# The row of sender scores of a graph-attention layer, turned in 32x32 squares by VectorE

## The chip, the cores and the metric

The kernel runs on one core of one Trainium2 chip. The time is that of one execution on the device, in microseconds (us); three runs of the kernel before were taken, and their median counts. The profile is of one further execution; its span is what the hardware profiler saw on that core. Busy times, waits and durations below are of that execution.

The engines of the core are named as the profile names them: PE is TensorE (matmuls and transposes), PEld its loading of weights, DVE is VectorE, ACT is ScalarE, POOL is GpSimd, SP is SyncE, which here only issues DMA transfers.

## The reference

Four graph layers run one after another over 32 graphs of 512 nodes with 128 features each; each layer normalizes, computes and adds its result to x. Layer 0 is a graph convolution, layer 1 a gated graph network with five steps, layers 2 and 3 are graph attention. The change touches only layers 2 and 3. Layer 3, cut to what matters:

```python
h = jnp.einsum('bnf,fo->bno', x, w)
e_src = jnp.einsum('bno,o->bn', h, a_src)
e_dst = jnp.einsum('bno,o->bn', h, a_dst)
e = jax.nn.leaky_relu(e_src[:, :, None] + e_dst[:, None, :], negative_slope=NEG_SLOPE)
mask = (a > 0)[None, :, :]
e = jnp.where(mask, e, -jnp.inf)
alpha = jax.nn.softmax(e, axis=-1)
out = jnp.einsum('bij,bjo->bio', alpha, h)
```

Layer 2 is the same with an ELU behind it. For each graph, one of the two scores must stand along the free dimension, as a row of 512 numbers that is the same on all 128 partitions, while the other stands as one number per partition. The kernel takes exponentials of scores first, so that the leaky ReLU of a sum becomes a maximum of two factors.

## The kernel before

The whole program is a list of operations, each with an engine, an estimated cost and a due time. A planner orders them ahead of time with these estimates; it tries sixteen settings of its ordering rule and keeps the one that ends first by its own estimates. Each engine then runs its operations in that fixed order, waiting on semaphores where data or buffers need it.

```python
def run(self):
    ...
    best = min(self.ends, key=lambda end: self.attempt(uses, *end))
    self.attempt(uses, *best)
    ...
    for o in self.order:
        o.emit()
```

The buffers that the change touches, and some of their neighbours:

```python
P = 128
W = 32
Q = P // W
NEAR = 4
...
"bank": tiles(8, TOKENS, "bank", psum),
...
"h_gat": tiles(3, [P, C, D + 3], "h_gat"),
"four": tiles(2, [Q, P], "four"),
"row": tiles(2, [P, N], "row"),
"line": tiles(4, [C, Q, W], "line", dram),
"e": tiles(2, [P, C, N], "e"),
```

`four` and `row` lie in the on-chip memory, `line` in device memory, `bank` in the matmul accumulator memory. C is 4, N is 512 and D is 128.

An attention layer of one graph makes the head tile `h_gat`: per node 128 features and three exponentials of scores in columns 128 to 130. Matmuls give features and scores (line 678), ACT takes the exponentials (line 680), and DVE multiplies the features by one of them (line 688). For the last four graphs ("near") other operations are used; those are not changed.

```python
def gat(b, l, due):
    ...
    near = b >= B - NEAR
    ...
    for a, q in enumerate(qs):
        ...
        op("PE", 2 * MM1, due + 1.5, heads, r=[gT, w_aug[l]], w=[*qs, h] if a == 0 else [q])
        op("ACT", 0.1, due + 1, lambda qt=qt, ht=ht: nc.scalar.activation(ht()[:, :, D:D + 3], qt()[:, :, D:D + 3], AF.Exp),
           r=[q], w=[h[2 + a]])
        if near:
            ...
        else:
            op("DVE", 0.335, due + 1.5, lambda qt=qt, ht=ht: nc.vector.tensor_mul(
                ht()[:, :, :D], qt()[:, :, :D], ht()[:, :, D:D + 1].to_broadcast([P, 2, D])), r=[q, h[2 + a]], w=[h[a]])
    exps = [h[2], h[3]]
```

Then the scores of column 130 are turned into a row. For the 28 graphs that are not near, PE transposes the four columns into four partitions of a bank (line 705), ACT copies them (line 707), one DMA writes them to `line` (line 708) and a second reads `line` back as a row on all partitions (line 710). DVE then makes the weighted mask `e` (line 713), and PE multiplies with it (line 733).

```python
    if near:
        ...
    else:
        pr, four, line = Val("bank"), Val("four"), Val("line")
        op("PE", 0.12, due + 1.5, lambda: nc.tensor.transpose(flat(pr.t)[:Q, :P], h.t[:, :, D + 2], ident.t),
           r=[*exps, ident], w=[pr, four])
        op("ACT", 0.22, due + 1.5, lambda: nc.scalar.copy(four.t, flat(pr.t)[:Q, :P]), r=[pr], w=[four])
        op("SP", 0.4, due + 1.5, lambda: nc.sync.dma_start(
            line.t.rearrange("c q i -> q c i"), four.t.rearrange("q (c i) -> q c i", c=C)), r=[four], w=[line], delay=2.5)
        op("SP", 0.4, due + 1.5, lambda: nc.sync.dma_start(
            row.t, line.t.rearrange("c q i -> (c q i)").unsqueeze(0).to_broadcast([P, N])), r=[line], w=[row, e], delay=7)
    for j in range(C):
        op("DVE", 0.68, due + 3, lambda j=j: nc.vector.scalar_tensor_tensor(
            e.t[:, j, :], row.t, h.t[:, j, D + 1:D + 2], maskT[l].t[:, j, :], op0=ALU.max, op1=ALU.mult),
           r=[row, h[2 + j // 2], maskT[l]], w=[e[j]])
```

Two layers and 28 graphs make 56 such rows.

Of the kernel before, what the change touches and what calls it, by code (L numbers as in the profile page):

```python
# [15 lines left out]
P = 128  # L16
# [3 lines left out]
W = 32  # L20
Q = P // W
# [23 lines left out]
class Plan:  # L45
# [8 lines left out]
    def op(self, engine, cost, due, emit, r=(), w=(), delay=None):  # L54
        o = Op(engine, cost, due, emit, self.DELAY[engine] if delay is None else delay)
        o.id = len(self.ops)
        before = {}
        for items, writes in ((r, False), (w, True)):
            for item in items:
                v, parts = item if isinstance(item, tuple) else (item, None)  # L60
                parts = range(len(v.writers)) if parts is None else [parts]
                if v not in o.vals:
                    o.vals.append(v)
                    v.uses += 1
                for c in parts:
                    before.update((p.id, p) for p in v.writers[c])
                    if writes:
                        before.update((p.id, p) for p in v.readers[c])
        for items, writes in ((r, False), (w, True)):
            for item in items:  # L70
                v, parts = item if isinstance(item, tuple) else (item, None)
                for c in range(len(v.writers)) if parts is None else [parts]:
                    if writes:
                        v.writers[c], v.readers[c] = [o], []
                    else:
                        v.readers[c].append(o)
        before.pop(o.id, None)
        for p in before.values():
            p.then.append(o)
        o.waits = len(before)  # L80
        self.ops.append(o)
# [86 lines left out]
def gnn_stack(ctx: ExitStack, tc: tile.TileContext, a: dict, out: bass.AP):  # L168
    nc = tc.nc
    x, adj = a["x"], a["adj"]  # L170
    B, N, D = x.shape
    C = N // P
# [6 lines left out]
    def tiles(n, shape, name, pool=sb, dtype=F32):  # L179
        return [pool.tile(shape, dtype, name=f"{name}_{next(serial)}") for _ in range(n)]  # L180

    def flat(t):
        return t.rearrange("p c k -> p (c k)")
# [18 lines left out]
        "hv": tiles(2, TOKENS, "hv"),  # L202
        "gT": tiles(2, [P, Q, W * C], "gT"),
        "h_gat": tiles(3, [P, C, D + 3], "h_gat"),
        "four": tiles(2, [Q, P], "four"),
        "row": tiles(2, [P, N], "row"),
        "line": tiles(4, [C, Q, W], "line", dram),
        "e": tiles(2, [P, C, N], "e"),
# [9 lines left out]
    op = plan.op  # L218
# [3 lines left out]
    def fixed(shape, name, parts=1, dtype=F32):  # L222
        v = Val(None, parts)
        v.t = tiles(1, shape, name, dtype=dtype)[0]
        return v
# [13 lines left out]
    ident = fixed([P, P], "ident")  # L239
# [8 lines left out]
    for c in range(C):  # L248
        e, q = (("SP", nc.sync), ("ACT", nc.scalar))[c % 2]
        op(e, 0.45, -1001, lambda c=c, q=q: q.dma_start(adj_sb.t[:, c, :], adj[c * P:(c + 1) * P, :]),  # L250
           w=[adj_sb[c]], delay=3.6)
    xs = []
    for b in range(B):
        v = Val("x", C)
        op("SP", 0.95, max(-995 + b, STEPS * b - 20) if b >= 8 else -995 + b, lambda v=v, b=b: nc.sync.dma_start(v.t, x[b].rearrange("(c p) d -> p c d", p=P)),
           w=[v], delay=3)
# [23 lines left out]
    for c in range(C):  # L280
        p = Val("bank")

        def turn_adj(c=c, p=p):
# [5 lines left out]
           r=[adj_sb[c]], w=[deg[c]])  # L289
# [17 lines left out]
    for m in range(C):  # L307
        op("DVE", 0.7, -797, lambda m=m: nc.vector.scalar_tensor_tensor(
            anT.t[:, m, :], adjT.t[:, m, :], dinv.t[:, m:m + 1], flat(drow.t), op0=ALU.mult, op1=ALU.mult),
           r=[adjT, dinv, drow], w=[anT[m]])  # L310
        op("DVE", 0.26, -797, lambda m=m: nc.vector.scalar_tensor_tensor(
            block(anT.t, m), ident.t, dinv2.t[:, m:m + 1], block(anT.t, m), op0=ALU.mult, op1=ALU.add),
           r=[ident, dinv2], w=[anT[m]])
# [19 lines left out]
    for l in (2, 3):  # L333
# [13 lines left out]
        for c in range(C):  # L347
            op("SP", 0.4, 4 + l, lambda l=l, c=c, far=far: nc.sync.dma_start(
                maskT[l].t[c * W:(c + 1) * W], far.t[:, :, c, :].rearrange("q i n -> i q n")),
               r=[far], w=[maskT[l][c]], delay=2.2)  # L350
# [33 lines left out]
    for k, u, half in (("w4", "u3", True), ("w3", "u3", True), ("w5", "u5", False)):  # L384
        gate_b[k] = fixed([P, 1], "gate_b" + k)
        op("DVE", 0.1, -14, lambda k=k, u=u: nc.vector.tensor_add(gate_b[k].t, raw["b" + k].t, raw["b" + u].t),
           r=[raw["b" + k], raw["b" + u]], w=[gate_b[k]])
# [4 lines left out]
    for i, l in enumerate((2, 3)):  # L392
        p = Val("bank")
        op("PE", 0.3, -9, lambda i=i, l=l, p=p: nc.tensor.matmul(p.t[:, 0, :2], gats.t[:, i, :], a_pair[l].t, start=True, stop=True),
           r=[gats, a_pair[l]], w=[p])
# [259 lines left out]
    def gat(b, l, due):  # L655
        xb, y, gT, h = xs[b], Val("y", C), Val("gT"), Val("h_gat", 4)
# [3 lines left out]
        if near:  # L660
# [4 lines left out]
               r=[pT], w=[gT])  # L665
# [6 lines left out]
        for a, q in enumerate(qs):  # L672
# [3 lines left out]
            def heads(a=a, qt=qt):  # L676
# [4 lines left out]
               r=[q], w=[h[2 + a]])  # L681
# [8 lines left out]
        exps = [h[2], h[3]]  # L690

        row, e = Val("row"), Val("e", C)
        if near:
            pr = Val("bank")

            def spread():
                for k in range(Q):
                    nc.tensor.transpose(pr.t[:, k, :], h.t[:, k, D + 2:D + 3].to_broadcast([P, P]), ident.t)
            op("PE", C * TURN, due + 2, spread, r=[*exps, ident], w=[pr, row])
            op("ACT", A, due + 2, lambda: nc.scalar.copy(  # L700
                row.t.rearrange("p (c q i) -> p c q i", c=C, q=Q), pr.t.rearrange("p q (c i) -> p c q i", c=C)),
               r=[pr], w=[row, e])
        else:
            pr, four, line = Val("bank"), Val("four"), Val("line")
            op("PE", 0.12, due + 1.5, lambda: nc.tensor.transpose(flat(pr.t)[:Q, :P], h.t[:, :, D + 2], ident.t),  # L705
               r=[*exps, ident], w=[pr, four])
            op("ACT", 0.22, due + 1.5, lambda: nc.scalar.copy(four.t, flat(pr.t)[:Q, :P]), r=[pr], w=[four])
            op("SP", 0.4, due + 1.5, lambda: nc.sync.dma_start(
                line.t.rearrange("c q i -> q c i"), four.t.rearrange("q (c i) -> q c i", c=C)), r=[four], w=[line], delay=2.5)
            op("SP", 0.4, due + 1.5, lambda: nc.sync.dma_start(  # L710
                row.t, line.t.rearrange("c q i -> (c q i)").unsqueeze(0).to_broadcast([P, N])), r=[line], w=[row, e], delay=7)
        for j in range(C):
# [3 lines that stand above are left out]
# [31 lines left out]
        if l == 2:  # L747
# [3 lines left out]
               r=[xb], w=[v])  # L751
            op("DVE", V, due + 4, lambda: nc.vector.scalar_tensor_tensor(flat(xb.t), flat(n.t), 1.0, flat(v.t), op0=ALU.min, op1=ALU.add),
               r=[n, v], w=[xb])
# [4 lines left out]
    for b in range(0, B, 2):  # L758
        gcn((b, b + 1), STEPS * b - 10)
        ggnn((b, b + 1), STEPS * b)  # L760
        for i in range(2):
            gat(b + i, 2, STEPS * (b + i) + LANES * (STEPS - 1) + 3)
            gat(b + i, 3, STEPS * (b + i) + LANES * (STEPS - 1) + 8)
# [32 lines left out]
```

The softmax here doesn't subtract the row's maximum and nothing guards it: scores larger than these inputs give would overflow.

## Time and profile before

| what | value |
|---|---|
| median of three runs | 1648.0 us (1646.48 to 1648.28) |
| span of the profiled execution | 1645.1 us |
| PE busy | 1620.7 us (99%) |
| DVE busy | 1373.5 us (83%) |
| ACT busy | 722.0 us (44%) |
| POOL busy | 144.6 us (9%) |
| mean granted clock of TensorE | 0.999 of full speed |

Busy time is the union of an engine's instructions, so that two matmuls that overlap in the pipeline are counted once. The table of stages gives, for stretches of the span, the busy time of each engine and in brackets the number of instructions in the stretch. In the table of groups a line holds the source line, the engine, the operation, the tiles written and read, their shapes and the count; behind the first bar stand the total busy time in us and the mean duration in ns, behind the second the idle time of the engine just before these instructions and what ended it. The chain that ended last is followed from the last instruction back to whatever released it.

### The profile page before, as it was taken

The page shows a single profiled execution, that of the slowest core. Times are in us where ns is not written, and L with a number is a line of the kernel's source. Part 1 is how long each engine was busy: PE and PEld are TensorE (multiplying, and loading weights), DVE is VectorE, ACT ScalarE, POOL GpSimd, SP SyncE. Part 2 cuts the span into 40 slices and gives each one's busy share as a digit, 9 for nine tenths or more (in the row PEclk, how much of TensorE's full clock was granted, in tenths as well). Part 3 has the DMA queues.
Part 4 walks back from the last instruction along what each step waited for, and adds up shares of the span by engine and source line. Part 5 has one row for each costly group of instructions (what it writes and reads, how often), then busy time and mean ns, then how long its engine had stood idle before and what let it go on. Part 6 is the DMA issues. An engine that isn't in the chain of part 4 may idle for free.

```text
span 1645.1 us, 23871 instructions
## 1 busy us (share of the span) xinstructions
PE 1620.7 (99%) x7306; PEld 1159.8 (71%) x7306; DVE 1373.5 (83%) x3881; ACT 722.0 (44%) x1629; POOL 144.6 (9%) x136
## 2 busy tenths in 40 slices
PE   8999999999999999999999999999999999999997
PEld 5666666777767677776776677767777777666776
DVE  8977587888878898888888898888888887788887
ACT  4643353534345443544534444353443534443433
POOL 2200010110101110000100100110000000000000
PEclk9999999999999999999999999999999999999999
DMA  5433253444535344453434535334363422434100
GB/s 148 109 73 72 53 127 93 104 106 105 124 78 136 90 106 106 102 134 86 113 95 100 129 90 142 87 94 113 91 143 76 114 68 72 122 91 103 46 20 26
DMA packets 381312, 159.81 MB, mean 97 GB/s; under 512 B 206976, under 2 KB 362752, under 8 KB 381184
## 3 DMA queue, kind: packets, MB, share of 16 engines
q1 hardware_dynamic: 380896, 157.77, 39.4%
q8 instruction: 58, 0.95, 0.2%
q14 instruction: 70, 0.57, 0.1%
q10 hardware_dynamic: 288, 0.52, 0.1%
HBM read 87.30 MB, written 70.89 MB: 96 GB/s over the span
## 4 chain that ended last, share of the span: by engine, by line
PE 94%; DVE 4%; DMA 1%; issue 0%; ACT 0%; SPq 0%; DVEq 0%
PE bank L516 34%; PE bank L733 12%; PE bank L603 8%; PE bank L604 8%; PE bank L617 8%; PE bank L610 8%; PE bank L618 8%; PE bank L678 3%; PE bank L572 1%; PE bank L722 1%; DVE e L713 1%; DVE st L406 1%; PE bank L705 0%; PE bank L448 0%; DVE y L432 0%
## 5 line engine op out<-in xcount | busy, mean ns | idle before, releaser
L413 POOL TENSOR_TENSOR rstd<-ve,mhalf 128x4 f32<-128x4 f32 x128 | 142.8, 1117 | 1473.4 <-DVE ve L411 1166.1
L516 PE MATMUL bank<-made,S 128*128 128x256 f32 x1128 | 270.3, 380 | 1.6 <-DVE S L504 0.7
L516 PEld LDWEIGHTS bank<-made,S 128*128 128x128 f32 x1128 | 217.3, 196 | 42.2 <-issue 18.6
L733 PEld LDWEIGHTS bank<-h_gat,e 128*128 128x128 f32 x1792 | 208.2, 192 | 17.4 <-issue 14.8
L521 ACT COPY half<-bank 128x256 f32<-128x256 f32 x282 | 104.6, 371 | 246.6 <-PE bank L516 239.1
L733 PE MATMUL bank<-h_gat,e 128*128 128x129 f32 x1792 | 209.0, 275 | 0.0
L606 ACT ACTIVATE r<-bank,gate_bw 128x512 f32<-128x512 f32 x160 | 109.6, 685 | 205.2 <-PE bank L604 186.5
L713 DVE SCALAR_TENSOR_TENSOR e<-row,h_gat,maskT 128x512 f32<-128x512 f32 x256 | 182.7, 742 | 0.0
L608 DVE SCALAR_TENSOR_TENSOR rh<-r,hT 128x512 f32<-128x512 f32 x160 | 109.9, 687 | 76.5 <-ACT r L606 75.6
L622 DVE TENSOR_TENSOR hv<-hv,hT 128x512 f32<-128x512 f32 x160 | 109.6, 685 | 75.9 <-ACT hv L620 75.3
L620 ACT ACTIVATE hv<-bank,gate_bw 128x512 f32<-128x512 f32 x160 | 109.5, 684 | 126.7 <-PE bank L618 125.6
L610 PE MATMUL bank<-m,wT 128*128 128x512 f32 x320 | 163.8, 593 | 0.0
L617 PE MATMUL bank<-m,wT 128*128 128x512 f32 x320 | 163.7, 593 | 0.0
L603 PE MATMUL bank<-m,wT 128*128 128x512 f32 x320 | 163.5, 592 | 0.0
L618 PE MATMUL bank<-rh,wT 128*128 128x512 f32 x320 | 163.4, 592 | 0.0
L604 PE MATMUL bank<-hT,wT 128*128 128x512 f32 x320 | 163.4, 592 | 0.0
L516 PE MATMUL bank<-adjT,h 128*128 128x256 f32 x640 | 161.6, 380 | 0.6 <-ACT h L423 0.3
L529 DVE TENSOR_TENSOR m<-half,bank 128x256 f32<-128x256 f32 x282 | 116.1, 413 | 33.2 <-ACT half L521 15.7
L516 PEld LDWEIGHTS bank<-adjT,h 128*128 128x128 f32 x640 | 121.2, 196 | 26.7 <-issue 11.3
L612 ACT ACTIVATE z<-bank,gate_bw 128x512 f32<-128x512 f32 x160 | 109.3, 683 | 53.8 <-PE bank L610 51.5
L406 DVE BATCH_NORM_STATS2 st<-x 128x6 f32<-128x128 f32 x512 | 121.5, 279 | 1.5 <-DMA x<-in_x_dram 0.6
L423 ACT ACTIVATE y<-x,off,rstd 128x128 f32<-128x128 f32 x240 | 104.5, 485 | 26.9 <-DVE off L420 25.0
(117 smaller groups left out, 2182.5 us busy)
## 6 DMA issues: line engine op xcount, KB each, us to landing
far<-sq SPq DMA_DIRECT2D x936, 64.0 KB
h<-far SPq DMA_DIRECT2D x248, 128.0 KB
gT<-far SPq DMA_DIRECT2D x56, 256.0 KB
row<-line SPq DMA_DIRECT2D x56, 256.0 KB
x<-in_x_dram SPq DMA_DIRECT2D x32, 256.0 KB
out_dram<-x SPq DMA_DIRECT2D x32, 256.0 KB
h<-far SPq DMA_DIRECT2D x28, 256.0 KB
hT<-far SPq DMA_DIRECT2D x104, 64.0 KB
```

The source lines that it names most:

```text
L406: op("DVE", 0.21, due, lambda c=c: nc.vector.bn_stats(st.t[:, c, :], xb.t[:, c, :]), r=[xb[c]], w=[st[c]])
L413: op("POOL", 1.0, due, lambda: nc.gpsimd.tensor_tensor(rstd.t, ve.t, mhalf.t, ALU.pow), r=[ve, mhalf], w=[rstd])
L516: nc.tensor.matmul(low(r), u[:, l, :], factors[k][0]()[:, l, :], start=fresh and l == 0, stop=l == 1, skip_group_check=not fresh)
L529: op("DVE", HV, due - 5, lambda: nc.vector.tensor_add(out(), u.t, low(t)), r=[u, t], w=[o])
L603: nc.tensor.matmul(flat(gate.t), gates.t[:, 0, :], flat(m.t), start=True, stop=False)
L604: nc.tensor.matmul(flat(gate.t), gates.t[:, 1, :], flat(hT.t), start=False, stop=True)
L608: op("DVE", V, due - 5, lambda: nc.vector.scalar_tensor_tensor(flat(rh.t), flat(r.t), 1.0, flat(hT.t), op0=ALU.add, op1=ALU.mult), r=[r, h ...
L610: op("PE", MM, due + 0.3, lambda: nc.tensor.matmul(flat(gate.t), gates.t[:, 2, :], flat(m.t), start=False, stop=True, skip_group_check=Tru ...
L617: nc.tensor.matmul(flat(cand.t), gates.t[:, 3, :], flat(m.t), start=True, stop=False)
L618: nc.tensor.matmul(flat(cand.t), u5T.t[:, 0, :], flat(rh.t), start=False, stop=True)
L713: op("DVE", 0.68, due + 3, lambda j=j: nc.vector.scalar_tensor_tensor(e.t[:, j, :], row.t, h.t[:, j, D + 1:D + 2], maskT[l].t[:, j, :], op ...
L733: nc.tensor.matmul(pt()[:, c, :D + 1], e.t[:, j, i * P:(i + 1) * P], h.t[:, j, :D + 1], start=(j == 0), stop=(j == C - 1))
```

## The change

One PE transpose and one ACT copy per row give way to one DVE instruction. DVE turns each 32x32 square of its operand by itself. It gets the last 32 columns (99 to 130) of each of the four slices of the head tile, 128 partitions by 4 x 32 numbers. Column 130, the score, is the last of its square, so it becomes the last row of each turned square, on partitions 31, 63, 95 and 127. Each of those four partitions then holds 128 scores side by side, and the first DMA takes these four partitions alone. The tile `four` grows from 4 x 128 to 128 x 4 x 32 numbers. The instruction reads feature columns too (99 to 127), whose turned values nobody uses, so it names the whole head tile as its input where the transpose named the exponentials alone. It is meant to free PE and ACT, and a bank, of this work.

```diff
-        "four": tiles(2, [Q, P], "four"),
+        "four": tiles(2, [P, Q, W], "four"),
...
         else:
-            pr, four, line = Val("bank"), Val("four"), Val("line")
-            op("PE", 0.12, due + 1.5, lambda: nc.tensor.transpose(flat(pr.t)[:Q, :P], h.t[:, :, D + 2], ident.t),
-               r=[*exps, ident], w=[pr, four])
-            op("ACT", 0.22, due + 1.5, lambda: nc.scalar.copy(four.t, flat(pr.t)[:Q, :P]), r=[pr], w=[four])
+
+            four, line = Val("four"), Val("line")
+            op("DVE", 0.2, due + 1.5, lambda: nc.vector.transpose(
+                four.t, h.t[:, :, D + 3 - W:]), r=[h], w=[four])
             op("SP", 0.4, due + 1.5, lambda: nc.sync.dma_start(
-                line.t.rearrange("c q i -> q c i"), four.t.rearrange("q (c i) -> q c i", c=C)), r=[four], w=[line], delay=2.5)
+                line.t, four.t[W - 1::W]), r=[four], w=[line], delay=2.5)
             op("SP", 0.4, due + 1.5, lambda: nc.sync.dma_start(
                 row.t, line.t.rearrange("c q i -> (c q i)").unsqueeze(0).to_broadcast([P, N])), r=[line], w=[row, e], delay=7)
```

## The prediction, made before the changed kernel was run

> **What bounds the kernel now.** I read the page's shares of busy time and its chain that ended last first, because they say which engine to charge and which to credit.
>
> ```profile
> PE 1620.7 (99%) x7306; PEld 1159.8 (71%) x7306; DVE 1373.5 (83%) x3881; ACT 722.0 (44%) x1629; POOL 144.6 (9%) x136
> PE 94%; DVE 4%; DMA 1%; issue 0%; ACT 0%; SPq 0%; DVEq 0%
> ```
>
> The first line is the busy time of each engine, the second the share of each in the chain. PE holds 94% of the chain and is idle for only 1645.1 - 1620.7 = 24.4 us. The next question is where those 24.4 us lie, so I cut the span into stages (stretch and its length, then busy us and instructions per engine, then the TensorE clock, the DMA share and GB/s).
>
> ```profile
> 0.00:50.00 50.00, 42.55 (x163) 27.37 (x164) 40.92 (x172) 27.53 (x64) 12.53 (x18) 1.00 0.54 149
> ...
> 400.00:600.00 200.00, 200.00 (x919) 144.56 (x918) 172.69 (x496) 87.81 (x198) 20.25 (x17) 1.00 0.44 106
> 600.00:800.00 200.00, 200.00 (x904) 143.93 (x903) 172.91 (x489) 88.81 (x201) 17.70 (x16) 1.00 0.45 109
> ...
> 1600.00:1645.10 45.10, 32.88 (x272) 30.67 (x272) 36.52 (x118) 14.24 (x44) 4.92 (x4) 0.97 0.08 24
> ```
>
> From 400 to 800 us PE has no idle time at all, at full clock, while DVE is at 172.7 of 200 us (86%). The idle time of PE is in the first 50 us (7.5 us) and the last 45 us (12.2 us). So in the middle, where nearly all 56 rows are made, an instruction taken from PE shortens the run, and one added to DVE need not lengthen it. Then the groups of the two operations that go.
>
> ```profile
> L705 PE MATMUL bank<-ident,h_gat 128*4 128x128 f32 x56 | 15.3, 272 | 0.0
> L707 ACT COPY four<-bank 4x128 f32<-4x128 f32 x56 | 13.8, 246 | 10.9 <-PE bank L705 10.1 <-DMA hT<-far 0.8
> ```
>
> The 15.3 us are a trap: 272 ns is the time of one transpose from start to end in the pipeline, and the next matmul starts before it ends. What it costs PE is the time to the next start. The order of time shows that (start us, length us).
>
> ```profile
> 708.28 1.02 PE L618 MATMUL bank<-rh,wT 128*128 128x512 f32 x2
> 709.14 0.27 PE L705 MATMUL bank<-ident,h_gat 128*4 128x128 f32 x1
> 709.25 1.02 PE L610 MATMUL bank<-m,wT 128*128 128x512 f32 x2
> 710.11 1.10 PE L617 MATMUL bank<-m,wT 128*128 128x512 f32 x2
> ```
>
> From 709.14 to 709.25 is 0.11 us; at 233.26, 763.39, 875.68 and 1573.77 us, four others that I looked at, the step is 0.11 us as well. The pair ahead of it takes 0.86 us from start to start (708.28 to 709.14), as the pair behind it does (709.25 to 710.11), so no pause for loading weights hides around the transpose.
>
> **What the Trainium skill says.** "Perfetto Trace Analysis", section Identifying the Most-Contended Engine, warns that matmul busy time is a poor measure, because matmuls are pipelined. The trace agrees: 272 ns of duration against 110 ns of cost. "TensorE: Matmul & The Clock Gate", section Part 4: PE-mode transpose, gives about 275 ns for a transpose inside a kernel and says that its output goes to PSUM, so that a copy must follow. The trace has 272 ns, and the copy is line 707; a lower clock around transposes, which the section also tells of, isn't seen here (1.00 in each middle stage). "VectorE: DVE Perf Modes", section The three transpose paths, says that DVE turns 32x32 blocks only, straight into SBUF, and gives 311 ns for 128x128 in bf16. The trace of before has no 128x128 case in fp32, but two larger ones, below; they lead to about the same. "DMA: Bandwidth & Descriptors", section Specifications, puts the smallest transfer at full rate at 512 B. The first DMA of a row goes from 16 pieces of 128 B to 4 of 512 B; no run here shows what that is worth, and 56 transfers of 2 KB are little beside the 159.81 MB of the page, so I give it nothing.
>
> **The change part by part.**
>
> *Removed from PE:* 56 transposes x 0.11 us = 6.2 us. They lie on the path that sets the end, since PE is the chain around them. This I count in full.
>
> *Removed from ACT:* 56 copies x 0.246 us = 13.8 us. ACT is at 44%, and no PE time of note waits for this copy, since a DMA is what reads it. Counted as 0.
>
> *Added to DVE:* 56 turns of 128 x 128 numbers. The profile has the same operation at two sizes.
>
> ```profile
> L462 DVE STREAM_TRANSPOSE sq<-y 128x512 f32<-128x512 f32 x56 | 39.3, 702 | 3.1 <-ACT y L423 2.9
> L458 DVE STREAM_TRANSPOSE sq<-hT 128x256 f32<-128x256 f32 x248 | 106.3, 434 | 0.7
> ```
>
> The slope is (702 - 434) / 256 = 1.05 ns for a column, so 128 columns take 434 - 134 = 300 ns. 56 x 0.30 = 16.8 us, and DVE goes from 1373.5 to about 1390 us. In a middle stage of 200 us there are 8 rows: DVE rises by 8 x 0.30 = 2.4 us, from 172.7 to 175.1 of 200, while PE falls by 0.9. DVE stays second. The planner is told 0.2 us for this instruction, a third too little; but it is told too little for other DVE work as well (0.61 for additions that take about 0.68), and PE has no waits all the same. I charge 0.7 us of new PE waits, which is a choice: some 4% of what is added to DVE.
>
> *Moved:* the turn waits for the multiplication of line 688 too, not for the exponentials alone. That is 0.41 us per half on the same engine and before it in order, so the row starts some tenths of a us later than it could; against that the step through PE and ACT (0.27 + 0.25 us) falls away. The reader of the row is line 713.
>
> ```profile
> L713 DVE SCALAR_TENSOR_TENSOR e<-row,h_gat,maskT 128x512 f32<-128x512 f32 x256 | 182.7, 742 | 0.0
> ```
>
> Its idle time is 0.0: DVE never stood before it waiting for a row. Some tenths of a us move nothing.
>
> *Sum:* -6.2 + 0.7 = -5.5 us, so 1648.0 - 5.5 = 1642.5 us.
>
> **The rivals.** (1) *DVE becomes the bound.* If all 16.8 us of DVE came onto the path, the change would cost 16.8 - 6.2 = 10.6 us: about 1658.6 us. For it: DVE is already at 86% in the middle, runs in a fixed order, and its own waits (75.6 us for line 606's result, 75.3 us for line 620's) come from loops through PE and ACT, so that its free time is not all usable. Against it: PE has not a us of idle time in the middle, so its work is ready ahead of time, and 2.4 us in 200 is little. (2) *The new order.* The planner orders everything anew, and the end can come out otherwise. The last 45 us hold 12.2 us of PE idle time and a long stretch of DVE in the chain, none of it changed directly, since the near graphs don't use this code. Another order could lengthen or shorten that by some 4 us, my guess from the size of single waits there (3.07 us before line 722 at 1623 us). That makes 1638 to 1647 us. The kernel before was tuned with its own order, so a new one is likelier worse than better at the ends. (3) *The work on PE was hidden anyway.* Then nothing changes: 1648. PE at 200.00 of 200 us speaks against it.
>
> **Range and chances.** The centre is the sum. The low end of the range is 6.2 us saved plus a tail some 6 us better: 1636. The high end is half of rival 1 or a bad tail: 1651. Even rival 1 whole is +0.6%, and 2% would be 33 us, twice all the DVE time added. So same within 2% gets 0.975, slower 0.015, faster 0.01.
>
> **What would show it.** Right: no line 705 and 707; PE busy about 6 us lower; the new instruction near 300 ns x56; DVE busy near 1390 us; PE still at 200 of 200 us in the middle stages. Wrong: PE idle time of several us in the middle with DVE as the releaser (rival 1); a last stretch with more than some 16 us of PE idle time (rival 2); a turn far longer than 300 ns, since its input is four strided pieces; DVE waiting for the row at line 713.

## The result, and the profile after

The changed kernel takes 1642.6 us (median of six runs, 1641.3 to 1644.9), against 1648.1 us of six runs of the kernel before: a ratio of 0.9971, 95% interval 0.9958 to 0.9984. That is 5.6 us less, where 5.5 were predicted. The experiments below show that the number came out right for only part of the reasons given.

The page of the kernel after, its shares of busy time and its chain that ended last:

```profile
PE 1617.2 (98%) x7250; PEld 1163.2 (71%) x7250; DVE 1378.8 (84%) x3937; ACT 715.6 (44%) x1573; POOL 144.0 (9%) x136
PE 94%; DVE 4%; DMA 1%; SPq 0%; issue 0%; ACT 0%; DVEq 0%
```

PE has 56 instructions fewer and is still the chain. Its busy time fell by 3.5 us and not by 6, and DVE's rose by 5.3 us and not by 16.8. The stages of the kernel after (same columns as before):

```profile
400.00:600.00 200.00, 200.00 (x901) 145.10 (x900) 172.89 (x492) 87.28 (x194) 18.17 (x17) 1.00 0.43 104
600.00:800.00 200.00, 200.00 (x894) 143.92 (x893) 173.60 (x499) 87.87 (x192) 18.01 (x17) 1.00 0.46 109
800.00:1000.00 200.00, 198.51 (x889) 143.16 (x888) 174.39 (x501) 88.66 (x196) 17.76 (x16) 1.00 0.44 107
...
1600.00:1643.00 43.00, 32.44 (x256) 31.18 (x254) 32.30 (x100) 12.54 (x38) 4.01 (x3) 0.91 0.09 25
```

and the third of these stages in the kernel before:

```profile
800.00:1000.00 200.00, 200.00 (x887) 142.84 (x886) 173.06 (x494) 92.64 (x212) 17.95 (x17) 1.00 0.44 107
```

PE now stands idle for 1.5 us between 800 and 1000 us, where before it had none. One wait for line 529 of DVE makes 1.3 us of that; over the whole run PE waits for it four times (us in total, times, longest us):

```profile
PE bank L516 <- DVE m L529: 3.2, 4, 1.4
```

In the last stage the TensorE clock is 0.91, where before it was 0.97. The groups of the new instruction and of the reader of the row:

```profile
L706 DVE STREAM_TRANSPOSE four<-h_gat 128x128 f32<-128x128 f32 x56 | 16.6, 296 | 0.7
...
L713 DVE SCALAR_TENSOR_TENSOR e<-row,h_gat,maskT 128x512 f32<-128x512 f32 x256 | 182.7, 741 | 0.0
```

The turn takes 296 ns in the mean, as worked out, and DVE still never waits for a row ahead of line 713. But 296 ns is the length of one turn, not what it costs DVE. The order of time on DVE shows that (start us, length us):

```profile
232.38 0.70 DVE L462 STREAM_TRANSPOSE sq<-y 128x512 f32<-128x512 f32 x1
233.00 0.27 DVE L706 STREAM_TRANSPOSE four<-h_gat 128x128 f32<-128x128 f32 x1
233.20 0.12 DVE L420 SCALAR_TENSOR_TENSOR off<-mv,rstd 128x4 f32<-128x4 f32 x1
```

The next instruction starts 0.20 us after the turn. Over the 56 turns the median from start to next start is 0.235 us, with DVE's waits in it. The turn overlaps the instruction behind it, just as matmuls do.

For the readings below I split PE's time in another way. From each start of a PE instruction to the next I took off the usual step of its kind, the median between 200 and 1400 us of the kernel before: 429 ns for 128x512, 216 for 128x256, 112 for 128x128, 128x129 and 128x131 (and, taken over, for the four of 128x2), 109 for the transpose of line 705. The steps add up to the work, and what is left are pauses, stretches at a lower clock included. The work is 1609.2 us with the 56 transposes and 1603.1 us without. The pauses of the profiled executions, in us:

| kernel | first 200 us | 200 to 1400 us | from 1400 us | sum |
|---|---|---|---|---|
| before | 11.0 | 1.4 | 13.7 | 26.1 |
| after | 10.4 | 3.8 | 15.6 | 29.8 |

(Sums are rounded apart from their parts.) So 3.7 us of the 6.1 came back as pauses in this pair of executions. The pair is only 2.2 us apart (1647.0 and 1644.8 us), where the medians are 5.6 apart, so it shows the changed kernel at its slower end. Such pauses are only in part visible as idle time: an instruction of 272 ns whose successor could start after 110 ns covers a pause of up to 0.16 us.

### The profile page after: what moved, and what is told of

It reads as the page before. It is cut to its first block, busy times and chain, and to the rows that moved or that the text cites. A ratio compares the mean times of both kernels' runs of the same rounds, so it can differ in the third digit from the quotient of the medians.

```text
span 1643.0 us, 23716 instructions
## 1 busy us (share of the span) xinstructions
PE 1617.2 (98%) x7250; PEld 1163.2 (71%) x7250; DVE 1378.8 (84%) x3937; ACT 715.6 (44%) x1573; POOL 144.0 (9%) x136
## 4 chain that ended last, share of the span: by engine, by line
PE 94%; DVE 4%; DMA 1%; SPq 0%; issue 0%; ACT 0%; DVEq 0%
PE bank L516 33%; PE bank L733 12%; PE bank L617 8%; PE bank L618 8%; PE bank L610 8%; PE bank L603 8%; PE bank L604 8%; PE bank L678 3%; PE bank L722 2%; PE bank L572 1%; DVE st L406 1%; PE bank L448 1%; DVE S L504 0%; DVE m L529 0%; DMA e<-in_adj_dram 0%
## 5 line engine op out<-in xcount | busy, mean ns | idle before, releaser
L516 PEld LDWEIGHTS bank<-made,S 128*128 128x128 f32 x1128 | 217.2, 196 | 43.3 <-issue 15.6
L529 DVE TENSOR_TENSOR m<-half,bank 128x256 f32<-128x256 f32 x282 | 115.6, 411 | 25.7 <-PE bank L516 13.7
L618 PEld LDWEIGHTS bank<-rh,wT 128*128 128x128 f32 x320 | 60.8, 190 | 76.5 <-issue 67.2
```

Source lines behind the costliest of these rows:

```text
L516: nc.tensor.matmul(low(r), u[:, l, :], factors[k][0]()[:, l, :], start=fresh and l == 0, stop=l == 1, skip_group_check=not fresh)
L529: op("DVE", HV, due - 5, lambda: nc.vector.tensor_add(out(), u.t, low(t)), r=[u, t], w=[o])
L618: nc.tensor.matmul(flat(cand.t), u5T.t[:, 0, :], flat(rh.t), start=False, stop=True)
```

## The experiments

The planner orders everything anew when an operation or its estimated cost changes, so "after" differs from "before" in the change and in the order of everything else. The first four kernels, and two later ones, keep the order: the operations stay in the plan as they were before, and only what they emit is altered.

**The change in the order of before.**

```diff
-"four": tiles(2, [Q, P], "four"),
+"four": tiles(2, [P, Q, W], "four"),
-op("PE", 0.12, ..., lambda: nc.tensor.transpose(flat(pr.t)[:Q, :P], h.t[:, :, D + 2], ident.t), ...
+op("PE", 0.12, ..., lambda: None, ...
-op("ACT", 0.22, ..., lambda: nc.scalar.copy(four.t, flat(pr.t)[:Q, :P]), ...
+op("ACT", 0.22, ..., lambda: nc.vector.transpose(four.t, h.t[:, :, D + 3 - W:]), ...
```

and the first DMA takes `four.t[W - 1::W]`.

> The order of all other work is that of the kernel before: the PE transpose is left out at its place and the DVE turn stands where the ACT copy stood; nothing is planned anew. My theory (56 transposes at 0.11 us of PE time come off a PE that is never idle, DVE has room): about 6 us less than before, 1641 to 1643 us. Rival, the DVE time comes onto the path: 1648 us or more, up to 1659. Rival, the gain of the change came from its new order and not from PE: about 1648 us, no gain.

Measured: 1646.1 us against 1647.2 us of before, ratio 0.9989 (0.9982 to 0.9996). Only 1.1 us came, not 6, and no range of the expectation holds 1646.1 us; the third, no gain, is the nearest. By the medians the change in the old order is worth little, and most of what "after" gained came with its new order. How far the clock enters here stands further down, under the clock at the end.

**The removal alone.** The row is then filled from numbers of the head tile as they lie, so this kernel leaves out the making of the right row.

```diff
-op("PE", ..., lambda: nc.tensor.transpose(...), ...
+op("PE", ..., lambda: None, ...
-op("ACT", ..., lambda: nc.scalar.copy(...), ...
+op("ACT", ..., lambda: None, ...
-    ... four.t.rearrange("q (c i) -> q c i", c=C)), r=[four], ...
+    ... h.t[:Q, 0, :D].rearrange("q (c i) -> q c i", c=C)), r=[four], ...
```

> The transpose and the copy are left out and nothing takes their place: the first DMA reads 4 x 128 numbers of the head tile as they lie, so that the row holds wrong numbers. It gives the worth of the removal by itself, in the order of before. My theory: 56 x 0.11 = 6.2 us less than before, about 1642 us, and no more than 1 us below the kernel with the turn in the held order. If DVE's turns cost anything, this kernel is faster than that one by that much: with all 16.8 us of DVE on the path, by 16.8 us.

Measured: 1643.6 us, ratio 0.9976 (0.9967 to 0.9985). Taking 6.1 us of work from PE brings 3.6 us. The DVE turn then costs 1646.1 - 1643.6 = 2.5 us of the path; since the intervals of the two ratios nearly touch (0.9985 and 0.9982), this is known to about one us only. The expectation of at most 1 us for it is missed.

**The price of a PE transpose.**

```diff
-lambda: nc.tensor.transpose(flat(pr.t)[:Q, :P], h.t[:, :, D + 2], ident.t)
+lambda: [nc.tensor.transpose(flat(pr.t)[:Q, :P], h.t[:, :, D + 2], ident.t) for _ in range(4)]
```

> The kernel before with each transpose made four times into the same bank: 168 more PE transposes in the same order. My theory, 0.11 us of PE time each and all of it on the path: 18.5 us more, about 1666.5 us. If a transpose costs PE its whole 0.27 us: 46 us more. If such work is hidden in PE's waits: no change.

Measured: 1665.7 us, 18.5 us more than before (ratio 1.0111, 1.0097 to 1.0124). 18.5 / 168 = 0.110 us for each transpose (0.095 to 0.122 by the interval), as the step in the order of time said. Within that, work added to PE is paid in full.

**The price of a DVE turn.** Two kernels in the order of before, with each turn made twice and four times.

```diff
-lambda: nc.vector.transpose(four.t, h.t[:, :, D + 3 - W:])
+lambda: [nc.vector.transpose(four.t, h.t[:, :, D + 3 - W:]) for _ in range(4)]
```

> As the held order with the turn, but each turn is made four times, into the same tile: 168 more DVE instructions, by the trace after of 0.31 us each and some 0.2 to 0.3 us to the next start, 34 to 52 us of DVE. My theory: DVE then stands at about 90% in the middle, and I expect it to cost some 2 to 6 us against one turn, since its free time is in loops through ACT and PE. DVE as the bound already: 34 to 52 us more. DVE with room to spare: under 1 us more.

> The held order with each turn made twice. The kernels with none, one and four turns took 1643.6, 1646.1 and 1681.3 us, so the first 56 turns cost 2.5 us and the next 168 cost 35.2, some 11.7 for each 56. Theory, DVE had a little room, which the first turn used up: 9 to 13 us more than with one turn, 1655 to 1659 us. Rival, the cost rises slowly and the room ends later: under 5 us more, with the larger part of the 35.2 us in the third and fourth turn.

Measured: 1655.3 us with two turns (ratio 1.0045, 1.0032 to 1.0057) and 1681.3 us with four (1.0203, 1.0189 to 1.0217). The first turn costs 2.5 us, the second 9.2, the third and fourth together 26.0. But a repeated turn takes more of DVE's time than a single one, as the order of time of the kernel with four shows:

```profile
415.81 1.35 DVE L707 STREAM_TRANSPOSE four<-h_gat 128x128 f32<-128x128 f32 x4
417.08 0.12 DVE L420 SCALAR_TENSOR_TENSOR off<-mv,rstd 128x4 f32<-128x4 f32 x1
```

Four turns of about 0.31 us take 1.35 us, so they don't overlap: each writes the same tile as the one before it and starts only after that has ended. Between two turns the step is 0.334 us in the mean with two turns and 0.343 us with four; the instruction behind the last one starts 0.236 us after it (median). The repeats therefore took some 56 x 0.334 = 18.7 us of DVE with two turns and 168 x 0.343 = 57.6 us with four, and cost 9.2 and 35.2 us, about half and three fifths; the single turn, some 13 us in all, cost 2.5. DVE's time is paid in part, and in a larger part the more of it there is.

The expectation for two turns held in its number. The one for four, written first, named 2 to 6 us as mine and was far too low. The 34 to 52 us that it gave for DVE as the bound contain the result, but they came from 0.2 to 0.3 us for each turn; all of the added time would have been 57.6 us. A stage of the kernel with four turns:

```profile
400.00:600.00 200.00, 195.42 (x879) 139.42 (x878) 174.78 (x500) 79.77 (x178) 17.52 (x15) 1.00 0.44 105
```

DVE's busy time in the stage is 174.8 of 200 us and PE waits; before it was 172.7 and PE did not. DVE is not full even so: in the whole run it waits 62.3 us for line 606's result and 65.7 us for line 620's (before: 75.6 and 75.3). The share of busy time thus does not say how much work an engine can still take. Where PE waits is shown by a group of the kernel before and two of this one:

```profile
L516 PE MATMUL bank<-made,S 128*128 128x256 f32 x1128 | 270.3, 380 | 1.6 <-DVE S L504 0.7 <-ACT half L521 0.5 <-DVE m L529 0.5
...
L516 PE MATMUL bank<-made,S 128*128 128x256 f32 x1128 | 274.0, 382 | 10.7 <-DVE m L529 6.9 <-ACT half L521 3.2 <-DVE S L504 0.4
L516 PEld LDWEIGHTS bank<-made,S 128*128 128x128 f32 x1128 | 216.4, 196 | 57.3 <-issue 17.5 <-DVE m L529 13.0 <-ACT half L521 6.8
```

PE's matmuls of line 516 and their weight loads wait for DVE's line 529, which adds partial products out of a bank. For line 529 the matmuls waited 0.5 us before and 6.9 us here. The pauses of this kernel from 200 to 1400 us sum to 34.3 us (before: 1.4), but its idle time in the stage above is only 4.6 us and its pauses there 7.3: busy time hid 2.7 us.

**A narrower turn.** The four slices can give 8 columns each to one square, so that DVE turns 128 x 32 numbers; column 130 then comes out on 16 partitions.

```diff
+"four": tiles(2, [P, W], "four"),
+lambda: nc.vector.transpose(four.t.rearrange("p (q k) -> p q k", q=Q), h.t[:, :, D + 3 - 8:])
+    ... line.t.rearrange("c q i -> (c q) i"), four.t[7::8]), r=[four], ...
```

> The held order with a narrower turn: of each slice of the head tile only the last 8 columns, the four slices side by side in one 32x32 square, so that DVE turns 128 x 32 numbers, and the first DMA takes 16 partitions of 128 B each. An instruction of some 0.2 us and near 0.1 us to the next start, against 0.31 and 0.23. Theory, the 2.5 us between none and one turn are DVE time: half of them or so comes back, 1644.3 to 1645.4 us. Rival, they come from the wait for the whole head tile or from the DMA: no change, 1646 us.

Measured: 1643.8 us against 1647.3 us of before, ratio 0.9977 (0.9970 to 0.9984), the same within noise as with no turn at all (0.9976), and under the range of the theory. The group of the wide turn in the order of before, and of this one:

```profile
L707 DVE STREAM_TRANSPOSE four<-h_gat 128x128 f32<-128x128 f32 x56 | 16.8, 301 | 0.5
...
L707 DVE STREAM_TRANSPOSE four<-h_gat 128x32 f32<-128x32 f32 x56 | 11.2, 200 | 0.5
```

The length fell from 301 to 200 ns, the median from start to next start from 0.23 to 0.13 us. The loss thus goes when DVE's time goes. The pauses of PE from 200 to 1400 us agree in the profiled executions: 3.3 us with no turn, 3.6 with the narrow one, 4.8 with the wide one, 12.6 with two and 34.3 with four. The wait for the whole head tile, which this kernel has as well, costs nothing that shows, and neither does its DMA of 16 pieces.

**Other orders of the same work.** One number of the planner altered, the instructions left as they are: for the turn 0.3 and 0.1 us in place of 0.2, and in the kernel before 0.14 and 0.10 us for the transpose in place of 0.12.

```diff
-op("DVE", 0.2, due + 1.5, lambda: nc.vector.transpose(
+op("DVE", 0.3, due + 1.5, lambda: nc.vector.transpose(
```

> The changed kernel with one number of the planner altered: it is told 0.3 us for the turn in place of 0.2, so it orders everything anew with the same work. My theory (the order matters little, the PE work decides): within 3 us of the changed kernel, 1640 to 1646 us. If the order matters as much as the change does: off by 5 us or more to one side.

> The changed kernel with 0.1 us told to the planner for the turn: a third order of the same work. My theory: 1640 to 1646 us, like the other two. If the order matters as much as the change does: off by 5 us or more to one side.

> The kernel before with 0.14 us told to the planner for the transpose in place of 0.12: another order of the work of before. My theory: within 3 us of the kernel before, 1645 to 1651 us, so that orders with the transpose lie above orders without. If the order of before was a lucky or an unlucky one: off by 5 us or more.

> The kernel before with 0.10 us told to the planner for the transpose: a third order of the work of before. My theory: 1645 to 1651 us. If the order of before was a lucky or an unlucky one: off by 5 us or more.

Measured, with the ratio to the kernel before:

| order | with the PE transpose | with the DVE turn |
|---|---|---|
| as given | 1647.2 us, 1 | 1642.6 us, 0.9971 (0.9958 to 0.9984) |
| higher estimate | 1649.4 us, 1.0012 (1.0005 to 1.0018) | 1647.7 us, 1.0000 (0.9992 to 1.0008) |
| lower estimate | 1644.2 us, 0.9978 (0.9970 to 0.9987) | 1646.0 us, 0.9990 (0.9982 to 0.9999) |

The orders of one kind of work spread over some 5 us, and a kernel with the transposes (1644.2) beats two without. My expectation that the two kinds would lie apart fell: 1647.7 and 1644.2 us lie outside their ranges, and the first is 5.1 us off, as the case in which the order matters had it. The means are 1646.9 and 1645.4 us, 1.5 us apart, near the 1.1 us of the held order; three orders on each side are too few to call that more than agreement.

**The clock at the end.** The stretches of the profiled execution of "after" in the last part (as above: busy us, instructions, then the clock in the third column from the end):

```profile
1616.00:1620.00 4.00, 0.84 (x5) 0.67 (x4) 3.93 (x21) 0.78 (x2) 1.72 (x2) 0.78 0.01 2
1620.00:1624.00 4.00, 4.00 (x21) 4.00 (x21) 3.31 (x10) 0.00 (x0) 0.80 (x1) 0.50 0.02 4
```

and PE in order of time around it:

```profile
1615.52 0.65 PE L698 MATMUL bank<-ident,h_gat 128*128 128x128 f32 x4 [0.48 <-ACT h_gat L685]
1619.33 3.81 PE L722 MATMUL bank<-h_gat,e 128*128 128x129 f32 x16 [3.16 <-DVE e L713]
```

PE waits 3.16 us for DVE, and then runs at half clock: 16 matmul instructions of 128x129 take 3.81 us. The Trainium skill, "TensorE: Matmul & The Clock Gate", section Why this matters for your kernels, warns of idle gaps over about 3 us, after which the clock falls to half; the trace agrees with 3.16 us and 0.50. But in the kernel before the same 16 instructions follow a wait of almost the same length at full clock:

```profile
1623.48 2.05 PE L722 MATMUL bank<-h_gat,e 128*128 128x129 f32 x16 [3.07 <-DVE e L713]
```

To test whether the wait matters, three matmuls that nobody reads fill the gap (the trace shows each as two instructions):

```diff
 def mix_from(j=j):
+    if (b, l, j) == (29, 3, 0):
+        for _ in range(3):
+            nc.tensor.matmul(flat(ps[1].t), ident.t, adjT.t[:, 0, :], start=True, stop=True)
```

> The changed kernel with three matmuls whose result nobody reads, put on PE ahead of the first mix of layer 3 of graph 29, where PE otherwise waits 3.3 us for VectorE and TensorE's clock then stands at half for 6.8 us. Theory, that wait brings the half clock and the half clock costs up to 3.4 us: the half-clock stretch goes, the wait is filled, and the time is 1640.5 to 1641.5 us. Rival, the half clock comes for another reason or hides beside VectorE's work: within 0.5 us of the changed kernel's 1642.6.

Measured: 1641.9 us, ratio 0.9963 (0.9951 to 0.9976). The same two views of the profiled execution:

```profile
1616.00:1620.00 4.00, 3.76 (x20) 2.28 (x19) 3.93 (x21) 0.00 (x0) 2.52 (x2) 1.00 0.01 2
1620.00:1624.00 4.00, 3.67 (x32) 3.36 (x31) 2.28 (x6) 1.80 (x5) 0.00 (x0) 1.00 0.02 4
```

```profile
1615.21 2.84 PE L723 MATMUL bank<-adjT,ident 128*128 128x512 f32 x6
1618.30 2.05 PE L725 MATMUL bank<-h_gat,e 128*128 128x129 f32 x16 [0.24 <-DVE e L713]
```

The wait is filled, the clock stays at 1.00, and the same 16 instructions take 2.05 us. Over the whole execution the mean granted clock is 0.999 or more in all five executions with the filling, and 0.998 in four of the six without. So filling the wait takes the half clock away here. Why the 3.07 us of before left the clock at 1.00, and what was different in the two executions of the changed kernel with 0.999 and 1.000, is not shown. The worth in time is not resolved: the median fell by 0.7 us, less than expected, and the two intervals overlap.

The same difference of clock runs through the comparisons above, since executions of one kernel differ in it and the medians mix them. At granted clocks of 0.997, 0.998 and 0.999 the change in the order of before is 2.9, 2.6 and 2.1 us faster than the kernel before, where the medians say 1.1: 10 of its 19 executions have 0.997, against 4 of 28. Between one turn and none 1.1 us (at 0.998) and 2.1 us (at 0.999) are left of the 2.5. Ahead of the last matmul the profiled executions of the three orders stand at half clock for 0, 10.2 and 0 us with the PE transpose and 6.8, 10.2 and 6.8 us with the DVE turn, in the table's sequence, of which at most half is lost (an estimate: half clock doubles the step). Whether the change, the order or chance brings these stretches was not tested, so the split of the gain between change and order is only known to some 2 us.

**Both together.**

> The changed kernel's order with both the narrow turn and the three filling matmuls. Theory, the two gains add up: 1 to 2 us under the one with the filling matmuls alone, so 1639 to 1640.5 us. If DVE's turn is hidden in this order: no difference from the one with the filling matmuls alone.

Measured: 1641.9 us, ratio 0.9966 (0.9953 to 0.9978). The narrow turn adds nothing in this order, though it saves some 2 us in the order of before; the expectation that the gains add up is missed. The last two kernels are the fastest of the study, level with each other, and their intervals overlap that of the changed kernel.

## Why the prediction was right, and where it was not

**The price of a transpose, 0.11 us: right.** Four transposes in place of one cost 0.110 us each.

**"They lie on the path that sets the end, since PE is the chain around them. This I count in full": half right.** The removal brought 3.6 us in the held order, not 6.2. Adding to PE is paid in full; taking away is not, since pauses grow. In the profiled executions the kernel without transposes and turns has 3.3 us of pauses from 200 to 1400 us, against 1.4 before. That PE gets ahead of the others there is a likely reason, not a shown one.

**The DVE turn at 300 ns: the length right, the cost wrong.** I warned of reading the length of a transpose on PE as its cost and then did just that on DVE: a single turn takes 0.20 to 0.235 us to the next start, some 13 us in all and not 16.8, so the 0.2 us told to the planner were nearly right. PE's and DVE's busy times, forecast 6 us lower and near 1390 us, moved less as well (3.5 us lower, 1378.8 us).

**"I charge 0.7 us of new PE waits": too small by 1.8 us.** It measured 2.5 us in the held order. The reason given, that PE at 200 of 200 us has its work ready ahead of time, doesn't hold: PE's busy time can't show pauses of up to 0.16 us. DVE at 86% took the narrow set of turns without a cost that shows; the wide set cost 2.5 us and a second wide one 9.2 us. So rival 1 was nearer than its place in the text says, and its sign, PE idle in the middle with DVE as the releaser, is there in small: the 1.3 us between 800 and 1000 us. In full, with all of DVE's time on the path, it didn't come even with four turns.

**The new order: its size right, its direction missed.** The guess of 4 us to either side fits the spread of 5 us over three orders. But a new order was called likelier worse, and this one was the best of its three. From held order to new order the time fell by a further 0.18% (0.9989 to 0.9971), about 3 us.

So the sum -6.2 + 0.7 should have read, for this order: -3.6 for the removal, +2.5 for DVE, and some -3 to -4 for the order and what comes with it, the clock included. The total is nearly the same by chance. Why this order is better than the other two stays open; in their profiled executions the pauses sum to 29.8 us for the order as given, 30.9 (lower estimate) and 31.9 (higher) for the two others, with the largest differences after 1400 us, where the half clock lies.

**Nothing for ACT, the moved wait and the DMA.** Line 713 waits for nothing, and the narrow turn with the same wait for the head tile costs nothing that shows, which fits. ACT's 13.8 us were never tested apart from PE's 6.1. Nor was the freed bank: the kernels in the order of before keep it set aside in the plan, so what it is worth would be part of the new order.

## What to carry to other kernels

An engine that is busy 100% of the time can still have pauses between its instructions; count steps from start to start, on every engine, before calling another engine free. Where a planner or compiler reorders everything at each change, measure the change once in the old order and a few other orders of the same work, or a gain of a few tenths of a per cent can't be told from the order. When work moves from the busiest engine to the second busiest, first make it small for its new place: in the old order the turn of 128 x 32 numbers cost nothing that showed, where that of 128 x 128 did. And where an instruction is repeated to find its price, see first whether the repeat takes the engine as long as the original: here it was 0.34 us against 0.235.

## What the runs showed of the hardware beyond that

SyncE takes longer to issue the first DMA of a row: a median of 270 ns before, from four neighbouring partitions, and 543 ns after, from partitions 31, 63, 95 and 127; the narrow turn's 16 partitions, 8 apart, take 528 ns. Fewer and longer pieces did not make the issue shorter. Whether the step between partitions is the cause was not tested; SyncE is not in the chain.
